# Rows that stay on chip in round three, scatters dealt out by ticks, and one transpose moved ahead of the last batch norm

## The chip, the cores and the metric

The kernel runs on one core of one Trainium2 chip. Its time is the device time of one execution in microseconds, here the median of the runs shown. A second kind of number is the time of one execution under the hardware profiler; that execution is the one that the profile shows, instruction by instruction.

## The reference

The input is x of shape (16, 1024, 128) in float32, a symmetric 0/1 adjacency of shape (16, 1024, 1024) with ones on its diagonal, and a node mask that is all ones. Two layers follow one another, both added to x:

```python
h = jnp.maximum(_layernorm(x, axis=-1), 0.0)
x = x + _L0_gnn_ref(h, adj, ...)        # masked attention: relu(softmax(q k^T on the edges) v Wo + bo)
h = jnp.maximum(_layernorm(x, axis=-1), 0.0)
x = x + _L1_gnn_ref(h, adj, nodemask, ...)
...
adj_d = _dilate(adj, mask)               # row by row, drops most edges of a node
h1 = _bn(relu(_sage(x, adj_d, Wr1, Wx1, b1, mf)), g1, be1)
h2 = _bn(relu(_sage(h1, adj_d, Wr2, Wx2, b2, mf)), g2, be2)
h3 = _bn(relu(_sage(h2, adj_d, Wr3, Wx3, b3, mf)), g3, be3)
return concatenate([h1, h2, h3]) @ Wl + bl
```

`_sage` takes the mean over the kept neighbours, multiplies by Wr, adds x Wx + b and divides each row by its norm. `_bn` normalises each of the 128 features over all 16 x 1024 rows. So there are three rounds, each needs the statistics of the whole round before it, and the last product needs those of round three.

## The kernel before

The work falls into four stages. A general path behind a flag is never taken with these inputs.

**Attention and dilation** come first and end at about 830 us of the profiled span. Beside the attention of one batch the dilation of the graph is solved. It finds the few nodes of a batch that keep any neighbour (at most 256 of 1024) and gives every node a slot, so that the nodes that keep neighbours come first. The 1024 rows of each batch are written to DRAM in the order of the slots, by eight indirect DMAs of 128 rows, and each row carries its node number along. `enter` (L861) reads that number into the tile `nodes`, with one small GpSimd copy for each batch (L864).

**Rounds one and two** then work on batches in slot order, feature by row (a batch is [128 features, 1024 rows]). Everything of round one is kept on the chip in eight tiles `r1` of two batches each, and that of round two in eight tiles `r2`. One batch is one run of the generator `mix` (L913): it makes the neighbour part for the first 256 rows (L918, L921), two half-batches of x Wx (`wx_half`, L937 and L938), adds the neighbour part (L956, L957), squares and sums (L947, L948), and scales by the norm (L959, L960, L963, L966). `turn` (L971) transposes the result back on TensorE (L976), ScalarE takes the relu (L982), and VectorE takes the statistics (L983). The transposes of one batch are issued during the next batch. `batchnorm` (L988) turns the statistics into scaled weights after each round, and `pieces` makes a row of bias for TensorE.

**Round three** does the same, and three things more, in the order that `in_turn` (L1009) is given by hand: `["mix", "thirds", "mix", "mix", "turn", "mix", "thirds", "turn"]`. After each of these eight items the clock ticks once, and what was put off with `later(n, ...)` is issued n ticks on. `thirds` multiplies the rows of rounds one and two by their thirds of Wl (L1114, L1115, into the PSUM tile `ph`), and VectorE adds x (tile `x2`, loaded by `load_rows` at L1100) and writes the sum into the second half of each row of the tile `y` (`add`, L986). The first half of `y` holds what `mix` gave (L966). `scatter_rows` then sends each group of 128 rows, both halves, 1024 bytes a row, to DRAM at the place of its node: eight indirect DMAs for a batch (`scatter`, L533, tile `y_d`), issued by GpSimd, one for each tick from the second tick after the batch. An `engine_nop` on GpSimd follows each. There are three buffers of `y`, so that batch b can start to fill its own only when the scatters of batch b-3 have been carried out. `load_back` (L1106) brings a batch back in node order into the same memory (`r2`, then `r1`): batch b/2 - 1 at every even b, and the last nine after the round, all on the queue of SyncE.

**The last product** follows the batch norm of round three. For every batch `raised` (L1155, L1160) transposes the first half of its rows and takes the relu, `final` multiplies it by the last third of Wl (L1167), adds the bias (L1168), VectorE adds that to the second half (L986 again), and SyncE stores the batch (L1171). The transposes of a batch are issued beside the product of the batch before it. Those of the first batch are issued after `batchnorm(2)` and `pieces` in program order.

```python
y = own.tile([P, NB, 2 * D], F32, name="y")
parts = {"mix": mix(b, r2[b // 2][:, b % 2, :], wxs, wrs, bias, rbias, y[:, :, :D]),
         "thirds": thirds(b, y)}
...
in_turn(["mix", "thirds", "mix", "mix", "turn", "mix", "thirds", "turn"], parts)
scatter_rows(b, y)
prev = (b, y[:, :, :D], None)
```

Of the kernel before, what the change touches and what calls it, by code (L numbers as in the profile page):

```python
# [15 lines left out]
P = 128  # L16
# [20 lines left out]
LAST = 12  # L37
GROUP = 4
# [473 lines left out]
def fast(ctx: ExitStack, tc: tile.TileContext, a, out, vp):  # L512
# [18 lines left out]
    def scatter(dst, slots, src, group):  # L531

        d = nc.gpsimd.indirect_dma_start(out=dst, out_offset=bass.IndirectOffsetOnAxis(ap=slots, axis=0),  # L533
                                         in_=src, in_offset=None)
        tc.declare_no_dep(d.ins, group=group, reason="the rows go to different places")
        tc.add_to_no_dep_group(group, d.ins)
        nc.gpsimd.engine_nop()
# [97 lines left out]
    with ExitStack() as s1:  # L635
# [225 lines left out]
        def enter(b):  # L861

            xt = XT.pop(b)
            nc.gpsimd.tensor_copy(nodes[:, b, :], xt[:, :, D].bitcast(I32))  # L864
# [48 lines left out]
    def mix(b, hT, wxk, wrk, bias, rbias, ob, on_scalar=False):  # L913
# [26 lines left out]
        def squares(g):  # L940
# [7 lines left out]
            later(2, lambda: nc.vector.tensor_reduce(n[:, 0, 4 * g:4 * g + 4], sq, axis=AX.X, op=OP.add))  # L948
# [31 lines left out]

    def put_off(b, g, pt, d):
        later(1, lambda: nc.scalar.activation(d, pt, AF.Relu))  # L982
        later(2, lambda: nc.vector.bn_stats(stats[:, 2 * b + g, :], d))  # L983

    def add(z, first, more):
        later(1, lambda: nc.vector.tensor_add(z, first, more))  # L986
# [83 lines left out]
    with big:  # L1070
# [20 lines left out]

        with tc.tile_pool(name="w3", bufs=3, reuse_waits="tile") as own:
# [3 lines left out]
            X2, R = {}, {}  # L1096
# [5 lines left out]
            def load_back(b):  # L1102

                R[b] = (r2 if b < B // 2 else r1)[b % (B // 2)].rearrange("p a n -> p (a n)").rearrange(
                    "p (k d) -> p k d", d=2 * D)
                nc.sync.dma_start(R[b], y_d[b].rearrange("(k p) d -> p k d", p=P))  # L1106

            def thirds(b, y):

                for g in range(2):  # L1110
# [5 lines left out]
                    add(y[:, 4 * g:4 * g + 4, D:], X2[b][:, 4 * g:4 * g + 4, :], pz)  # L1116
                    yield

            def scatter_rows(b, y):

                for k in range(NB):
                    later(2 + k, lambda k=k: scatter(y_d[b], nodes[:, b, k:k + 1], y[:, k, :], f"y_{b}"))
# [4 lines left out]
            for b in range(B):  # L1127
                if 0 < b < B - 1:
                    later(2, lambda b=b: load_rows(b + 1))
                if b % 2 == 0 and b:  # L1130
                    later(3, lambda b=b: load_back(b // 2 - 1))
                y = own.tile([P, NB, 2 * D], F32, name="y")
                parts = {"mix": mix(b, r2[b // 2][:, b % 2, :], wxs, wrs, bias, rbias, y[:, :, :D]),
                         "thirds": thirds(b, y)}
                if prev:
                    parts["turn"] = turn(*prev)
                in_turn(["mix", "thirds", "mix", "mix", "turn", "mix", "thirds", "turn"], parts)
                scatter_rows(b, y)
                prev = (b, y[:, :, :D], None)
            clock.flush()  # L1140
            drain(turn(*prev))
            clock.flush()
            for b in range(B // 2 - 1, B):
# [3 lines left out]
        (wl2,), pr = batchnorm(2, [wl[:, 2, :]])  # L1147
        bias, = pieces("pc3", [(zrow, pr[:, 0, :])], few)
        tall = big.enter_context(tc.tile_pool(name="w4", bufs=2, reuse_waits="tile"))

        def raised(b, hT):
            for g in range(2):
                pt = ps.tile([P, 4, P], F32, name="pt")
                for k in range(4):
                    nc.tensor.transpose(pt[:, k, :], R[b][:, 4 * g + k, :D], identf)  # L1155
# [3 lines left out]
        def raise_half(h, pt):  # L1159
            later(1, lambda: nc.scalar.activation(h, pt.rearrange("p a b -> p (a b)"), AF.Relu))  # L1160

        def final(b, h):
            for g in range(2):
# [5 lines left out]
                add(R[b][:, 4 * g:4 * g + 4, D:], R[b][:, 4 * g:4 * g + 4, D:], pz)  # L1169
                yield  # L1170
            later(2, lambda: nc.sync.dma_start(out[b].rearrange("(k p) d -> p k d", p=P), R[b][:, :, D:]))  # L1171

        h = tall.tile([P, N], F32, name="hT")
        drain(raised(0, h))
        clock.flush()
        for b in range(B):
            parts = {"final": final(b, h)}
            if b + 1 < B:
                h = tall.tile([P, N], F32, name="hT")
                parts["raised"] = raised(b + 1, h)  # L1180
            in_turn(["raised", "final", "raised", "final"], parts)
        clock.flush()
    return dil.flag
# [584 lines left out]
```

## Time and profile before

| what | us |
|---|---|
| median of 3 runs | 1262.63 (1258.08 to 1264.05) |
| the profiled execution, as a run | 1343.16 |
| its span in the profile | 1341.1 |
| attention, dilation and round one end at (first step of the batch norm) | about 940 |
| round two, until its batch norm | about 940 to 1038 |
| round three, from its first product to the batch norm after it | 1047.2 to 1269.9 |
| last product, first to last VectorE addition's end | 1278.6 to 1333.6 |
| end of the span | 1341.1 |

The profiled execution is 80.5 us longer than the median, so that its durations are those of a longer run than the one that is measured.

The page names a group of instructions by line, engine, operation, what it writes and what it reads, then how many there were, their busy time, the mean length of one in nanoseconds, and the idle time of their engine just before them with what ended most of it. "issue" means that nothing that the profile shows was waited for, and "remote" or "another core or an unknown queue" that the semaphore that ended the wait can't be tied to an instruction. TensorE has two rows, PE for products and PEld for the loading of weights. In a view of stretches of time, PEclk is the share of TensorE's full clock that was granted.

### The profile page before, as it was taken

Reading aid. Unit: us, or ns where it says so; the run is one execution under the profiler, and the core shown is the slowest. Engines: PE = TensorE matmul, PEld = TensorE weight load, DVE = VectorE, ACT = ScalarE, POOL = GpSimd, SP = SyncE. Lnnn points to the kernel's source line nnn. Section 1 sums busy time; section 2 is a strip of 40 time slices with the busy share of each in tenths; the row PEclk is TensorE's granted clock in tenths of the full one; section 3 lists DMA queues with packets and bytes.
Section 4 is the critical chain, followed back from the end, with each engine's and each line's share of the span. In section 5 each row is a group of like instructions: output and inputs, shape, how many; then the busy total and the mean of one; then the engine's idle time right before and its main releaser. Section 6 shows DMA issues by size and latency. Waiting matters only on the chain.

```text
span 1341.1 us, 22234 instructions
## 1 busy us (share of the span) xinstructions
PE 1138.2 (85%) x7815; PEld 854.3 (64%) x7815; DVE 882.6 (66%) x2630; ACT 732.2 (55%) x1580; POOL 548.1 (41%) x961
## 2 busy tenths in 40 slices
PE   4899899998899998998997976987798777777597
PEld 2577566666666666765665665765676666666585
DVE  6668567768776777767777785988587433434443
ACT  5578677767667776766776424665355212222232
POOL 0222464454445536426436156961000255555500
PEclk9899999999999998989999997998799788888899
DMA  6534334333334342433343014220000254444594
GB/s 211 151 121 127 110 119 135 127 111 115 122 111 131 123 143 91 130 123 95 115 125 108 21 52 112 82 65 1 0 1 20 80 163 147 150 146 150 173 342 142
DMA packets 117745, 153.92 MB, mean 115 GB/s; under 512 B 9196, under 2 KB 93048, under 8 KB 117624
## 3 DMA queue, kind: packets, MB, share of 16 engines
q1 hardware_dynamic: 105080, 118.65, 29.0%
q0 software_dynamic: 12544, 33.77, 7.4%
q8 instruction: 63, 1.03, 0.3%
q14 instruction: 58, 0.48, 0.1%
HBM read 118.63 MB, written 33.75 MB: 114 GB/s over the span
## 4 chain that ended last, share of the span: by engine, by line
PE 51%; DVE 23%; ACT 7%; issue 6%; POOL 5%; another core or an unknown queue 5%; DMA 3%; SPq 0%; POOLq 0%; DVEq 0%; ACTq 0%
PE ps L691 9%; PE po L707 9%; PE pm L670 6%; PE po L937 5%; DVE e L694 3%; DMA rows<-in_adj_dram,row 3%; PE ph L1167 2%; PE ph L1114 2%; DVE stats L983 2%; PE pt L976 2%; ACT e L693 2%; DVE left L304 2%; PE ph L1115 2%; PE pm L678 2%
## 5 line engine op out<-in xcount | busy, mean ns | idle before, releaser
L707 PEld LDWEIGHTS po<-vw,e 128*128 128x128 f32 x2048 | 276.4, 196 | 67.4 <-issue 67.0
L707 PE MATMUL po<-vw,e 128*128 128x129 f32 x2048 | 310.2, 286 | 0.0
L691 PE MATMUL ps<-qT,kT 128*128 128x512 f32 x512 | 273.4, 617 | 0.8 <-ACT e L693 0.8
L694 DVE TENSOR_TENSOR e<-e,ab 128x512 f32<-128x512 f32 x256 | 177.7, 695 | 125.3 <-ACT e L693 113.6
L533 POOL DMA_INDIRECT y_d<-y,nodes x128 | 123.2, 963 | 236.2 <-DVE y L966 193.3
L693 ACT ACTIVATE e<-ps 128x512 f32<-128x512 f32 x256 | 153.2, 598 | 120.3 <-PE ps L691 92.3
L533 POOL DMA_INDIRECT x_d<-xt,slot x128 | 141.7, 1107 | 38.7 <-issue 35.1
L166 ACT ACTIVATE ab<-st,d_one_k 128x1024 bf16<-128x1024 f32 x128 | 147.0, 1149 | 0.0
L570 POOL TENSOR_SCALAR ln_t<-ln_st 128x8 f32<-128x8 f32 x31 | 8.0, 259 | 289.3 <-DVE ln_st L563 232.0
L176 ACT ACTIVATE junk<-st 128x1024 bf16<-128x1024 f32 x112 | 118.4, 1057 | 0.0
L1114 PE MATMUL ph<-ws,r 128*128 128x128 f32 x256 | 63.5, 336 | 46.7 <-DVE y L986 45.7
L947 ACT ACTIVATE sq<-po 128x512 f32<-128x512 f32 x80 | 47.7, 596 | 88.2 <-PE po L938 67.2
L716 ACT ACTIVATE o<-po,recips 128x128 f32<-128x128 f32 x128 | 46.8, 368 | 73.3 <-DVE recips L714 69.7
L691 PEld LDWEIGHTS ps<-qT,kT 128*128 128x128 f32 x512 | 79.3, 195 | 7.6 <-issue 3.1
L1114 PEld LDWEIGHTS ph<-ws,r 128*128 128x128 f32 x256 | 49.3, 239 | 53.9 <-DVE y L986 48.5
L986 DVE TENSOR_TENSOR y<-x,ph 128x512 f32<-128x512 f32 x32 | 22.0, 688 | 89.4 <-remote 65.9
L937 PE MATMUL po<-ws,r 128*128 128x128 f32 x512 | 79.6, 303 | 0.0
L937 PEld LDWEIGHTS po<-ws,r 128*128 128x128 f32 x512 | 69.8, 211 | 12.7 <-issue 10.9
L582 POOL TENSOR_SCALAR hn<-xt,ln 128x128 f32<-128x128 f32 x120 | 76.4, 648 | 1.6
L948 DVE TENSOR_REDUCE nrm<-sq 128x4 f32<-128x512 f32 x80 | 54.1, 676 | 34.0 <-ACT sq L947 20.3
L191 DVE SCALAR_TENSOR_TENSOR junkv<-pd,ab 128x64 bf16<-128x64 int32 (+7 forms) x128 | 57.8, 452 | 18.2 <-PE pd L185 12.4
L582 POOL TENSOR_SCALAR hn<-xt 128x128 f32<-128x128 f32 x112 | 57.8, 528 | 27.1 <-PE pt L592 26.6
(292 smaller groups left out, 2382.4 us busy)
## 6 DMA issues: line engine op xcount, KB each, us to landing
st<-in_adj_dram SPq DMA_DIRECT2D x128, 512.0 KB
r<-y_d SPq DMA_DIRECT2D x16, 1024.0 KB
xt<-x_d SPq DMA_DIRECT2D x16, 524.0 KB
xt<-in_x_dram SPq DMA_DIRECT2D x16, 512.0 KB
x<-x_d SPq DMA_DIRECT2D x16, 512.0 KB
out_dram<-r SPq DMA_DIRECT2D x16, 512.0 KB
x_d<-xt,slot POOLq DMA_INDIRECT x128
y_d<-y,nodes POOLq DMA_INDIRECT x128
```

The lines of the kernel that those rows point to most:

```text
L166: nc.scalar.activation(ab[:, k, :], st, AF.Exp, bias=self.one_k, scale=ONE_K, accum_out=self.deg[:, b, k:k + 1])
L176: nc.scalar.activation(junk, st, AF.Exp, scale=-ZERO_K, accum_out=zeros)
L191: nc.vector.scalar_tensor_tensor(junk.rearrange("p a b -> p (a b)")[:, :n], pt.rearrange("p a b -> p (a b)").bitcast(I32)[:, :n], 1.0, ab[ ...
L533: d = nc.gpsimd.indirect_dma_start(out=dst, out_offset=bass.IndirectOffsetOnAxis(ap=slots, axis=0), in_=src, in_offset=None)
L582: engine.tensor_scalar(hn[:, k, :], xt[:, k, :D], minus[:, k // 2, k % 2, None], rstd[:, k // 2, k % 2, None], op0=OP.add, op1=OP.mult)
L670: nc.tensor.matmul(pp, w, hT[:, 512 * g:512 * g + 512], start=True, stop=True)
L691: nc.tensor.matmul(p, K[b][:, k * P:(k + 1) * P], Q[b][:, c], start=True, stop=True)
L693: later(1, lambda: nc.scalar.activation(e, p, AF.Exp))
L694: later(2, lambda: nc.vector.tensor_mul(e, e, AB_[b][:, k, c]))
L707: nc.tensor.matmul(po[:, q % 2, :], E[k][:, i * P:(i + 1) * P], V[b][:, k, :], start=(k == 0), stop=(k == NB - 1))
L937: nc.tensor.matmul(po[:, i, :], hT[:, c:c + P], wxk, start=(i == 3), stop=False)
L1114: nc.tensor.matmul(pz[:, i, :], r1[b // 2][:, b % 2, c], wl0, start=True, stop=False)
```

## The change

- Five batches, 2, 5, 8, 11 and 14 (`STAY`), are not scattered in round three. Their relu from `turn` goes into their part of `r2` in slot order, feature by row, and the sum of `thirds` into their part of `r1`. They are neither loaded back nor transposed again. In the last product their result is scattered straight to the output by eight indirect DMAs of 512-byte rows each. For these batches `nodes` holds the node number plus b times 1024, by `tensor_scalar` in place of the copy.
- The other eleven are scattered to `y_d` as before. `load_back` now fetches batch b-3 during batch b, in two DMAs of 512-byte pieces, into that batch's own part of `r2` and of `r1`.
- A scatter is no longer put off by a fixed number of ticks: it is put into a list, and `pace_scatters`, called after each tick, issues the first of the list if it is due and the number of the tick is no multiple of three. Ahead of each such scatter GpSimd copies one column from `last[0]`, a view of what VectorE wrote last in program order, into the tile `mark`. What is left in the list after the last tick is issued without that copy.
- In the last product the order of batches is 2, 0, 1, 5, 3, 4, 8, 6, 7, 11, 9, 10, 14, 12, 13, 15, and the transposes of batch 0, the first that needs any, stand ahead of `batchnorm(2)` in program order.

```diff
--- before.py
+++ after.py
@@ -35,6 +35,7 @@
 TICKS = 6 * NB
 GROUPS = ((0, 4, 5 * TICKS, 8 * TICKS), (4, 8, 9 * TICKS, 13 * TICKS), (8, 12, 13 * TICKS, 16 * TICKS))
 LAST = 12
+STAY = (2, 5, 8, 11, 14)
 GROUP = 4
 AB = 2
 ST = 3
@@ -528,12 +529,17 @@
     ones3 = consts.tile([3, P], BF, name="ones3")
     nc.vector.memset(ones3, 1.0)
 
-    def scatter(dst, slots, src, group):
+    def apart(d, own, *others):
+        for group in others:
+            tc.declare_no_dep(d.ins, group=group, reason="the rows go to different places")
+        tc.add_to_no_dep_group(own, d.ins)
+    def scatter(dst, slots, src, group, *others):
 
         d = nc.gpsimd.indirect_dma_start(out=dst, out_offset=bass.IndirectOffsetOnAxis(ap=slots, axis=0),
                                          in_=src, in_offset=None)
-        tc.declare_no_dep(d.ins, group=group, reason="the rows go to different places")
-        tc.add_to_no_dep_group(group, d.ins)
+        apart(d, group, group, *others)
         nc.gpsimd.engine_nop()
 
     def load_const(name, shape, src):
@@ -861,7 +867,8 @@
         def enter(b):
 
             xt = XT.pop(b)
-            nc.gpsimd.tensor_copy(nodes[:, b, :], xt[:, :, D].bitcast(I32))
+            nc.gpsimd.tensor_scalar(nodes[:, b, :], xt[:, :, D].bitcast(I32), float(b * N if b in STAY else 0), None, op0=OP.add)
             hT = work.tile([P, N], F32, name="hT", bufs=3)
             hn = work.tile([P, NB, D], F32, name="hn")
             halves = lambda c: xt[:, :, c].rearrange("p (a t) -> p a t", t=2)
@@ -945,7 +952,12 @@
                         sq[:, i, :], halves[g][:, i, :], AF.Square, accum_out=n[:, 0, 4 * g + i:4 * g + i + 1]))
                 return
             later(1, lambda: nc.scalar.activation(sq, halves[g], AF.Square))
-            later(2, lambda: nc.vector.tensor_reduce(n[:, 0, 4 * g:4 * g + 4], sq, axis=AX.X, op=OP.add))
+            def reduce():
+                nc.vector.tensor_reduce(n[:, 0, 4 * g:4 * g + 4], sq, axis=AX.X, op=OP.add)
+                last[0] = n[:, 0, 4 * g:4 * g + 1]
+            later(2, reduce)
 
         wx_half(1)
         squares(1)
@@ -978,12 +990,22 @@
             put_off(b, g, flat, flat if dst is None else dst[:, 512 * g:512 * g + 512])
             yield
 
+    last = [stats[:, 0, 0:1]]
     def put_off(b, g, pt, d):
+        def sums():
+            nc.vector.bn_stats(stats[:, 2 * b + g, :], d)
+            last[0] = stats[:, 2 * b + g, 0:1]
         later(1, lambda: nc.scalar.activation(d, pt, AF.Relu))
-        later(2, lambda: nc.vector.bn_stats(stats[:, 2 * b + g, :], d))
+        later(2, sums)
 
     def add(z, first, more):
-        later(1, lambda: nc.vector.tensor_add(z, first, more))
+        def one():
+            nc.vector.tensor_add(z, first, more)
+            last[0] = z[:, 0, 0:1]
+        later(1, one)
 
     def batchnorm(k, weights):
 
@@ -1089,11 +1111,30 @@
             clock.flush()
 
 
+        tall = lambda b: r2[b // 2][:, b % 2, :]
+        blocks = lambda t: t.rearrange("p (k d) -> p k d", d=D)
+        rows_r = lambda b: blocks(r2[b // 2][:, b % 2, :])
+        rows_z = lambda b: blocks(r1[b // 2][:, b % 2, :])
+        mark = few.tile([P, 1], F32, name="mark")
+        waiting, ticks3 = [], 0
+        def pace_scatters():
+            nonlocal ticks3
+            ticks3 += 1
+            if ticks3 % 3 and waiting and waiting[0][0] <= ticks3:
+                nc.gpsimd.tensor_copy(mark, last[0])
+                waiting.pop(0)[1]()
         with tc.tile_pool(name="w3", bufs=3, reuse_waits="tile") as own:
             (wxs, wrs, wl1), pr = batchnorm(1, [wx[2], wr[2], wl[:, 1, :]])
             bias, rbias = pieces("pc2", [(bs[2], pr[:, 0, :]), (None, pr[:, 1, :])], few)
             zrow = add_row(zrow, pr, 2)
-            X2, R = {}, {}
+            X2 = {}
 
             def load_rows(b):
                 X2[b] = own.tile([P, NB, D], F32, name="x2", bufs=2)
@@ -1101,11 +1142,11 @@
 
             def load_back(b):
 
-                R[b] = (r2 if b < B // 2 else r1)[b % (B // 2)].rearrange("p a n -> p (a n)").rearrange(
-                    "p (k d) -> p k d", d=2 * D)
-                nc.sync.dma_start(R[b], y_d[b].rearrange("(k p) d -> p k d", p=P))
-
-            def thirds(b, y):
+                if b not in STAY:
+                    for i, rows in enumerate((rows_r, rows_z)):
+                        nc.sync.dma_start(rows(b), y_d[b].rearrange("(k p) d -> p k d", p=P)[:, :, i * D:i * D + D])
+            def thirds(b, z):
 
                 for g in range(2):
                     pz = ps.tile([P, 4, P], F32, name="ph")
@@ -1113,13 +1154,12 @@
                         c = slice((4 * g + i) * P, (4 * g + i + 1) * P)
                         nc.tensor.matmul(pz[:, i, :], r1[b // 2][:, b % 2, c], wl0, start=True, stop=False)
                         nc.tensor.matmul(pz[:, i, :], r2[b // 2][:, b % 2, c], wl1, start=False, stop=True)
-                    add(y[:, 4 * g:4 * g + 4, D:], X2[b][:, 4 * g:4 * g + 4, :], pz)
+                    add(z[:, 4 * g:4 * g + 4, :], X2[b][:, 4 * g:4 * g + 4, :], pz)
                     yield
 
             def scatter_rows(b, y):
-
                 for k in range(NB):
-                    later(2 + k, lambda k=k: scatter(y_d[b], nodes[:, b, k:k + 1], y[:, k, :], f"y_{b}"))
+                    waiting.append((ticks3 + 2, lambda k=k: scatter(y_d[b], nodes[:, b, k:k + 1], y[:, k, :], f"y_{b}")))
 
             load_rows(0)
             load_rows(1)
@@ -1127,37 +1167,43 @@
             for b in range(B):
                 if 0 < b < B - 1:
                     later(2, lambda b=b: load_rows(b + 1))
-                if b % 2 == 0 and b:
-                    later(3, lambda b=b: load_back(b // 2 - 1))
+                if b >= 3:
+                    later(3, lambda b=b: load_back(b - 3))
                 y = own.tile([P, NB, 2 * D], F32, name="y")
                 parts = {"mix": mix(b, r2[b // 2][:, b % 2, :], wxs, wrs, bias, rbias, y[:, :, :D]),
-                         "thirds": thirds(b, y)}
+                         "thirds": thirds(b, rows_z(b) if b in STAY else y[:, :, D:])}
                 if prev:
                     parts["turn"] = turn(*prev)
-                in_turn(["mix", "thirds", "mix", "mix", "turn", "mix", "thirds", "turn"], parts)
-                scatter_rows(b, y)
-                prev = (b, y[:, :, :D], None)
+                in_turn(["mix", "thirds", "mix", "mix", "turn", "mix", "thirds", "turn"], parts, pace_scatters)
+                if b not in STAY:
+                    scatter_rows(b, y)
+                prev = (b, y[:, :, :D], tall(b) if b in STAY else None)
             clock.flush()
-            drain(turn(*prev))
+            for _ in turn(*prev):
+                clock.tick()
+                pace_scatters()
             clock.flush()
-            for b in range(B // 2 - 1, B):
+            while waiting:
+                waiting.pop(0)[1]()
+            for b in range(B - 3, B):
                 load_back(b)
 
 
-        (wl2,), pr = batchnorm(2, [wl[:, 2, :]])
-        bias, = pieces("pc3", [(zrow, pr[:, 0, :])], few)
-        tall = big.enter_context(tc.tile_pool(name="w4", bufs=2, reuse_waits="tile"))
+        talls = big.enter_context(tc.tile_pool(name="w4", bufs=3, reuse_waits="tile"))
 
         def raised(b, hT):
             for g in range(2):
                 pt = ps.tile([P, 4, P], F32, name="pt")
                 for k in range(4):
-                    nc.tensor.transpose(pt[:, k, :], R[b][:, 4 * g + k, :D], identf)
+                    nc.tensor.transpose(pt[:, k, :], rows_r(b)[:, 4 * g + k, :], identf)
                 raise_half(hT[:, 512 * g:512 * g + 512], pt)
                 yield
 
         def raise_half(h, pt):
             later(1, lambda: nc.scalar.activation(h, pt.rearrange("p a b -> p (a b)"), AF.Relu))
+        def scatter_out(b, k):
+            scatter(out.rearrange("b n d -> (b n) d"), nodes[:, b, k:k + 1], rows_z(b)[:, k, :], "out", "stores")
 
         def final(b, h):
             for g in range(2):
@@ -1166,20 +1212,37 @@
                     c = slice((4 * g + i) * P, (4 * g + i + 1) * P)
                     nc.tensor.matmul(pz[:, i, :], h[:, c], wl2, start=(i == 0), stop=False)
                 nc.tensor.matmul(pz.rearrange("p a b -> p (a b)"), ones3, bias, start=False, stop=True)
-                add(R[b][:, 4 * g:4 * g + 4, D:], R[b][:, 4 * g:4 * g + 4, D:], pz)
+                half = rows_z(b)[:, 4 * g:4 * g + 4, :]
+                add(half, half, pz)
+                if b in STAY:
+                    for k in range(4 * g, 4 * g + 4):
+                        waiting.append((ticks3 + 3, lambda k=k: scatter_out(b, k)))
                 yield
-            later(2, lambda: nc.sync.dma_start(out[b].rearrange("(k p) d -> p k d", p=P), R[b][:, :, D:]))
-
-        h = tall.tile([P, N], F32, name="hT")
-        drain(raised(0, h))
+            if b not in STAY:
+                later(2, lambda: apart(nc.sync.dma_start(out[b].rearrange("(k p) d -> p k d", p=P), rows_z(b)), "stores", "out"))
+        order = [b for i in range(0, B - 1, 3) for b in (i + 2, i, i + 1)] + [B - 1]
+        hs = {b: tall(b) for b in STAY}
+        def raise_next(i):
+            b = next((b for b in order[i:i + 2] if b not in hs), None)
+            if b is None:
+                return iter(())
+            hs[b] = talls.tile([P, N], F32, name="hT")
+            return raised(b, hs[b])
+        drain(raise_next(1))
         clock.flush()
-        for b in range(B):
-            parts = {"final": final(b, h)}
-            if b + 1 < B:
-                h = tall.tile([P, N], F32, name="hT")
-                parts["raised"] = raised(b + 1, h)
-            in_turn(["raised", "final", "raised", "final"], parts)
+        (wl2,), pr = batchnorm(2, [wl[:, 2, :]])
+        bias, = pieces("pc3", [(zrow, pr[:, 0, :])], few)
+        for i, b in enumerate(order):
+            parts = {"final": final(b, hs[b]), "raised": raise_next(i + 1)}
+            in_turn(["raised", "final", "raised", "final"], parts, pace_scatters)
         clock.flush()
+        while waiting:
+            waiting.pop(0)[1]()
     return dil.flag
 
 
```

## The prediction

> **What bounds the kernel now.** I read the page's chain of work first, then the groups of lines, then round three and the last product in order of time.
>
> ```profile
> PE 51%; DVE 23%; ACT 7%; issue 6%; POOL 5%; another core or an unknown queue 5%; DMA 3%; SPq 0%; POOLq 0%; DVEq 0%; ACTq 0%
> L533 POOL DMA_INDIRECT y_d<-y,nodes x128 | 123.2, 963 | 236.2 <-DVE y L966 193.3
> L986 DVE TENSOR_TENSOR y<-x,ph 128x512 f32<-128x512 f32 x32 | 22.0, 688 | 89.4 <-remote 65.9
> ```
>
> TensorE leads, but 5% of the chain hangs on semaphores that no instruction explains, and the third row says where: the addition of `thirds` in round three, 65.9 us over 15 waits. One such wait, in order of time:
>
> ```profile
> 1163.67 0.96 POOL L533 DMA_INDIRECT y_d<-y,nodes  x1 [0.30 <-issue]
> 1164.34 0.28 PE L921 MATMUL ph<-pc,ones 3*128 3x256 bf16 x1
> 1164.94 0.96 POOL L533 DMA_INDIRECT y_d<-y,nodes  x1 [0.30 <-issue]
> 1167.41 0.69 DVE L986 TENSOR_TENSOR y<-x,ph 128x512 f32<-128x512 f32 x1 [3.98 <-remote]
> 1167.47 0.58 ACT L982 ACTIVATE pt<-pt 128x512 f32<-128x512 f32 x1 [3.79 <-remote]
> 1168.16 0.49 PE L1114 MATMUL ph<-ws,r 128*128 128x128 f32 x2 [3.53 <-DVE y L986]
> 1169.82 0.96 POOL L533 DMA_INDIRECT y_d<-y,nodes  x1 [3.91 <-DVE y L966]
> ```
>
> TensorE has nothing left to do at 1164.6. VectorE and ScalarE both wait for its products, which ended by 1164, and both start together at 1167.4, half a microsecond after the last scatter's data. The period is 13.75 us (the additions at 1153.67, 1167.41, 1181.18). TensorE's own share is 8.59: two `thirds` of 1.785 each (1161.47 to 1163.26) and the 5.02 of a batch of round two (962.32 to 967.34). GpSimd's is 8 scatters of 0.96 + 0.30, so 10.1.
>
> The last product is TensorE's, end to end; with transposes a half-batch takes 1.80 us (1328.60 - 1326.80, the row before), without 1.41:
>
> ```profile
> 1328.60 0.97 PEld L1167 LDWEIGHTS ph<-ws,hT 128*128 128x128 f32 x8
> 1330.01 0.97 PEld L1167 LDWEIGHTS ph<-ws,hT 128*128 128x128 f32 x8 [0.23 <-issue]
> 1331.42 0.97 PEld L1167 LDWEIGHTS ph<-ws,hT 128*128 128x128 f32 x8 [0.23 <-issue]
> ```
>
> [...] after each wait PEclk is 0.50 for some 3 us, so that the first `thirds` takes 2.9 us (1154.41 to 1157.30) in place of 1.79, and the half-batch behind it 1.6 in place of 1.1. [...] here data still flows until 1166.9, 1 us after the row's end at 1165.9. [...] the trace shows small GpSimd operations of 0.20 us that at times take 1.10, but all 128 scatters of `y_d` within 0.957 to 1.019. [...]
>
> **Which time the sum is made against.** The profiled execution took 1343.2, 80.5 more than the median. Are the waits in the median too? Suppose not. They take 54.0 us of the chain in round three (23.9% of 226 from 1046 to 1272), and the half-clock after them about 1.65 x 15 = 25. Without them round three would be GpSimd's: the addition of batch 15 waits for `y`, so for the scatters of batch 12, which end at 1059.3 + 13 x 10.16 + 1.5 = 1192.9; then come 5.8 us of VectorE's rows for a batch and 3.6 of transposes, relu and statistics, and the batch norm starts at 1202.3 in place of 1269.9, 67.6 earlier. The other unexplained waits of the chain are 60.3 (4.5% of 1341.1) - 54.0 = 6.3. That gives 1269.3; were even GpSimd no bound, the batch norm would start at 1190.7 (1047.2 + 3.0 of half-clock + 16 x 8.59 - 1.7 that the first and last batch lack + 4.8 of tail) and the total be 1257.7. The median, 1262.6, lies between them, 6.7 below the one and 4.9 above the other. The rest of the kernel has no 80 us to give. So I take the waits for a cost of the profiled execution, and everything below for the median.
>
> **The change, part by part.**
>
> *Five batches not scattered.* 40 of 128 scatters leave round three. GpSimd needs 88 scatters and their copies. The price of a copy between two scatters stands in the dilation's own rows:
>
> ```profile
> 804.81 0.97 POOL L533 DMA_INDIRECT x_d<-xt,slot  x1 [0.30 <-issue]
> 805.81 0.20 POOL L864 COPY nodes<-xt 128x8 int32<-128x8 int32 x1
> 806.18 0.98 POOL L533 DMA_INDIRECT x_d<-xt,slot  x1 [0.17 <-issue]
> ```
>
> Start to start it is 1.37 in place of 1.27, since the copy fills a gap. Three batches now hold 16 scatters: 16 x 1.37 = 21.9, against 25.8 of TensorE. Round three becomes TensorE's. Gain: 1202.3 - 1190.7 = 11.6 at most, nothing if GpSimd was no bound before. The median's place between the two cases puts it at 4.9/11.6 of that, 4.9; scatters of late batches that nobody waited for may add some, so I take 7.
>
> *The pacing.* Two scatters in three ticks, so 2.74 us of GpSimd in 3.22. Each copy waits for VectorE's latest write; behind it on GpSimd only scatters are queued. Who waits for those: the `y` of three batches on, and `load_back`. For batches 1, 4, 7, 10, 13 the last scatter falls on tick 8b + 24 and batch b+3 needs `y` at tick 8b + 26, 2.15 us later. The scatter needs a lag of 1.37 behind its neighbour, 1.37 of its own and 1.5 of landing: VectorE then waits about 2 us. It has 8.59 - 5.8 = 2.8 to spare in a batch, and TensorE wants the PSUM tile `ph` of that addition again only five ticks on, so I cost it at nothing; uncovered it is 5 x 2 = 10 us. The range is 0 (a later `y` can't gain anything) to 10.
>
> *Loads.* 11 batches of two 0.5 MB loads for 16 of 1 MB. SyncE issues 22 x 0.36 for 16 x 0.46, hidden (SyncE is idle between). In a TensorE-bound batch 0.5 MB of `x2`, 0.69 of loads and 0.69 of scatters make 220 GB/s; 1272 to 1296 carried 345 to 380, so this hides. `load_back(1)` may wait a microsecond on SyncE for the scatter just named; the next `load_rows` is seven ticks off.
>
> *Stay batches on other engines.* Relu to SBUF 0.60 for 0.58, statistics from SBUF 0.687 for 0.698: nothing. `nodes` by `tensor_scalar`: 16 x about 0.02 to 0.2, hidden in round one, at most 3 us.
>
> *Last product.* Ten half-batches need no transposes: 10 x (1.80 - 1.41) = 3.9. The transposes ahead of the batch norm free TensorE from 1272.8 to 1275.5, but the bias row is there only at 1275.95 (L624), so its first half-batch ends at about 1276.3 in place of 1277.94: 1.6. Together 5.5, if TensorE stays the bound. Against it GpSimd: batch 15's eight scatters run until 8.7 us after the start of the batch norm, then 40 x 1.37 = 54.8, 1.0 of data and 3.6 that before lay between the last data (1337.5) and the end: 68.1 after that start. Before it was 71.2, TensorE now 65.7. So GpSimd ends last, and the gain is 3.1. Bounds: 5.5 down to -2.5 (each scatter like the mean of `x_d`, 1.107, which is 0.14 x 40 = 5.6 more).
>
> **Sum.** 7 + 3.1 = 10.1; 1262.6 - 10.1 = 1252.5, say 1252 (0.8%). The likeliest case's own range is 1245 to 1259. Half a per cent, 6.3 us, is about what can be told from no change.
>
> **Rivals.**
> *TensorE was the bound already (1258).* GpSimd's 0.30 gap may be the profile's too; round three then gives nothing and the last product 5. For it: 1257.7 above lies as near to the median. Against: the gaps are 0.30 wherever scatters follow each other.
> *The waits are real (about 1190).* Then pacing takes away up to 54 + 25, less if some stay: 1182 to 1230. For it: the chain. Against: the 80.5.
> *GpSimd becomes the bound (1273, slower).* Place: the last product and the pairs of scatters. Price: at c us each the end lies 8.7 + 40c + 4.6 after the batch norm's start, 2 us more for each 0.05. The 7 from round three are gone at c = 1.62, and half a per cent is lost from 1.78 on. At c = 2.0: 93.3 - 71.2 = 22 less at most 11.6, so +10. For it: scatters of `x_d` between VectorE's rows took up to 2.39. Against: those of `y_d` never over 1.02.
>
> **Chances.** Forecast 0.42, TensorE already 0.23, waits real 0.12, GpSimd 0.23. Faster: 0.36 of the first, 0.07 of the second, 0.12 = 0.55. Same: 0.06 + 0.16 + 0.02 = 0.24. Slower: 0.21. The range 1230 to 1275 leaves out most of the third case (0.10) and the far part of the fourth (0.09).
>
> **What would show it.** In the profile after: scatters of round three spaced and 88 in number, a period near 8.6 wherever no unexplained wait stands, no half-clock there; 40 scatters to the output about 1.37 apart, the last a few us after the last addition; the first products of the last stage right behind the batch norm's. It is wrong if GpSimd's rows are longer than 1.1 or if TensorE waits for VectorE's addition behind a wait for `y`.

## The result, and the profile after

| where | before | after | ratio, 95% interval |
|---|---|---|---|
| the timing of the change | 1260.17 us (6 runs) | 1249.33 us (6 runs) | 0.9908 [0.9886, 0.993] |

The change takes 10.8 us off, 0.9%; predicted were 10.1 and 1252. The total is right, but two terms of it are wrong in opposite directions, and the reason given for the level it is measured from is wrong. The experiments below fell on three chips, which are not alike, and no number can be read without that: on chip A the kernel before takes 1258 us, on chips B and C about 1346 (1338.5 to 1353.7 in all executions). B was used before and after A, so that the hour doesn't explain it; whether it is the chip itself, or something else that differs there, can't be told. The timing of the change was made where before takes 1260; the profile of before, 1343, looks like those of chips B and C.

The profiled execution after took 1249.27 us (span 1247.5), as its median. Groups of instructions of the profile after:

```profile
L540 POOL DMA_INDIRECT y_d<-y,nodes x88 | 86.4, 982 | 29.0 <-issue 28.5 <-DVE nrm L957 0.5
L540 POOL DMA_INDIRECT out_dram<-r,nodes x40 | 39.3, 981 | 7.2 <-issue 7.1 <-DVE r L1005 0.2
L1005 DVE TENSOR_TENSOR y<-x,ph 128x512 f32<-128x512 f32 x22 | 15.1, 688 | 9.2 <-PE ph L1156 6.7 <-POOL mark L1130 1.6
L1130 POOL COPY mark<-y 128x1 f32<-128x1 f32 x30 | 5.8, 193 | 145.8 <-DVE y L1005 143.0 <-DVE nrm L975 1.8 <-POOLq L543 0.4
```

The addition of `thirds` (third row) waits 9.2 us in all, and none of it is "remote", where before had 65.9. The scatters no longer wait for a batch's `y`. Of the copies' 145.8 us of waits (fourth row) 143.0 are a single one, until the first addition of round three; inside the round 18 of the other 79 copies show a wait for VectorE, of 0.2 to 0.5 us, 6.2 in all. GpSimd in round three, in order of time:

```profile
1099.47 0.99 POOL L540 DMA_INDIRECT y_d<-y,nodes  x1 [0.16 <-issue]
1100.83 0.18 POOL L1130 COPY mark<-stats 128x1 f32<-128x1 f32 x1 [0.37 <-DVE stats L997]
1101.49 0.98 POOL L540 DMA_INDIRECT y_d<-y,nodes  x1 [0.48 <-issue]
1102.50 0.19 POOL L1130 COPY mark<-r 128x1 f32<-128x1 f32 x1
1102.86 0.98 POOL L540 DMA_INDIRECT y_d<-y,nodes  x1 [0.16 <-issue]
1103.86 0.20 POOL L1130 COPY mark<-nrm 128x1 f32<-128x1 f32 x1
1104.50 0.98 POOL L540 DMA_INDIRECT y_d<-y,nodes  x1 [0.44 <-issue]
```

Half of the scatters follow the one before after 1.37 us (1101.49, 1102.86), nearly all others after 1.6 to 2.1. Counting as one train the scatters less than 1.45 us apart, round three of after has trains of one to five until its last batch, whose remainder, 13 scatters, runs past the batch norm; before had trains of eight, a batch each. The stretches of round three (second to third batch norm) in before and in after, with busy time of PE, PEld, DVE, ACT and POOL, TensorE's clock, DMA share and GB/s:

```profile
1038.80:1269.90 231.10, 168.30 (x1078) 149.02 (x1078) 94.68 (x179) 48.53 (x116) 117.68 (x123) 0.85 0.44 140
```

```profile
1021.00:1171.00 150.00, 141.27 (x1081) 124.78 (x1082) 94.62 (x179) 49.51 (x116) 93.97 (x160) 0.96 0.63 185
```

TensorE is busy 141 of 150 us at 0.96 of its clock: it bounds round three now, as predicted. The first row is from a profile like those of chips B and C, so the difference of 81 us is not the gain of the timing. The end of after:

```profile
1171.02 1.02 DVE L1013 BATCH_NORM_AGGREGATE bn<-stats 128x2 f32<-128x192 f32 x1
...
1180.48 0.96 POOL L540 DMA_INDIRECT y_d<-y,nodes  x1 [0.30 <-issue]
1182.85 0.18 POOL L1130 COPY mark<-r 128x1 f32<-128x1 f32 x1 [1.41 <-DVE r L1005]
1183.55 0.98 POOL L540 DMA_INDIRECT out_dram<-r,nodes  x1 [0.52 <-issue]
...
1232.12 0.69 DVE L1005 TENSOR_TENSOR r<-r,ph 128x512 f32<-128x512 f32 x1 [0.72 <-PE ph L1214]
...
1237.68 0.98 POOL L540 DMA_INDIRECT out_dram<-r,nodes  x1 [0.16 <-issue]
```

VectorE is done at 1232.8, GpSimd's last scatter at 1238.66, and the span ends at 1247.5, 8.8 later. In those 8.8 us the trace has two instructions of GpSimd that the view leaves out, INC_SWDGE_SEM from 1240.22 (1.39 us) and DRAIN from 1241.65 (4.98 us). In both before and after the pair runs behind GpSimd's last DMA, and I read it as the closing of GpSimd's DMA queue. In before (1.39 and 4.98 us as well) it ran from 1281.84 on, beside the last product.

### The profile page after: what moved, and what is told of

The parts are those of the page before. It is cut to its first block, busy times and chain, and to the rows that moved or that the text cites. A ratio compares the mean times of both kernels' runs of the same rounds, so it can differ in the third digit from the quotient of the medians.

```text
span 1247.5 us, 22348 instructions
## 1 busy us (share of the span) xinstructions
PE 1101.4 (88%) x7775; PEld 824.0 (66%) x7775; DVE 881.2 (71%) x2630; ACT 727.6 (58%) x1570; POOL 576.8 (46%) x1082
## 5 line engine op out<-in xcount | busy, mean ns | idle before, releaser
L713 PEld LDWEIGHTS po<-vw,e 128*128 128x128 f32 x2048 | 273.2, 194 | 65.8 <-issue 65.3
L713 PE MATMUL po<-vw,e 128*128 128x129 f32 x2048 | 307.0, 284 | 0.0
L540 POOL DMA_INDIRECT x_d<-xt,slot x128 | 144.2, 1127 | 38.8 <-issue 35.1
L540 POOL DMA_INDIRECT y_d<-y,nodes x88 | 86.4, 982 | 29.0 <-issue 28.5
L1000 ACT ACTIVATE r<-pt 128x512 f32<-128x512 f32 x74 | 44.4, 601 | 58.3 <-PE pt L988 58.3
L944 PE MATMUL po<-ws,r 128*128 128x128 f32 x512 | 75.4, 292 | 0.0
L305 DVE TENSOR_TENSOR_SCAN left<-rows 128x1024 f16<-128x1024 f32 x16 | 38.1, 2384 | 51.4 <-DMA rows<-in_adj_dram,row 51.4
L944 PEld LDWEIGHTS po<-ws,r 128*128 128x128 f32 x512 | 64.8, 198 | 12.8 <-issue 11.2
L1130 POOL COPY mark<-y 128x1 f32<-128x1 f32 x30 | 5.8, 193 | 145.8 <-DVE y L1005 143.0
L997 DVE BATCH_NORM_STATS2 stats<-r 128x6 f32<-128x512 f32 x74 | 50.9, 688 | 29.6 <-ACT r L1000 29.2
```

Source lines behind the costliest of these rows:

```text
L713: nc.tensor.matmul(po[:, q % 2, :], E[k][:, i * P:(i + 1) * P], V[b][:, k, :], start=(k == 0), stop=(k == NB - 1))
L944: nc.tensor.matmul(po[:, i, :], hT[:, c:c + P], wxk, start=(i == 3), stop=False)
```

## The experiments

The first batch norm's start, the time from the second batch norm to the third (round three) and that from the third to the end of the span (tail), in us from the traces ("paced" means that the copy into `mark` stands ahead of a scatter):

| chip | kernel | scatters of `y` in round three | first batch norm | round three | tail |
|---|---|---|---|---|---|
| (timing) | after | 88, paced | 923.6 | 149.8 | 76.5 |
| A | after | 88, paced | 927.0 | 150.0 | 74.1 |
| A | after, trains with gap | 88 | 924.1 | 150.0 | 73.6 |
| A | after without the copy | 88 | 922.1 | 149.9 | 75.1 |
| A | none stays | 128, paced | 919.8 | 173.2 | 89.3 |
| B | before, two profiles | 128 | 953.6, 946.6 | 232.3, 229.4 | 70.6, 70.0 |
| B | before, last store on GpSimd | 128 | 947.1 | 231.7 | 75.2 |
| C | before with gap | 128 | 939.6 | 227.1 | 73.2 |
| B | no pacing in round three | 88 | 942.5 | 209.5 | 84.8 |
| B | four stay, no copy | 96 | 951.3 | 213.3 | 84.7 |
| B | four stay | 96, paced | 945.3 | 153.7 | 95.2 |
| C | four stay | 96, paced | 944.3 | 151.6 | 90.9 |

Up to the first batch norm all of these kernels run nearly the same code, so this stretch compares the chips without the change. In it readers of TensorE's results have remote waits in all nine traces of the slower kind (eight on B and C, and the first profile of before), 2.6 to 16.7 us in each, every one of them beside a train of eight scatters of `x_d` (in before these start at most 1.8 us apart, and the waits end 0.8 to 2.4 us after the start of the eighth); in the five traces of A and of the timing, with the same trains, there is none. The longest group in before, with us in total, times, and the longest:

```profile
ACT kT L671 <- remote: 6.6, 4, 3.7
```

Round two, in which GpSimd scatters nothing, takes the same everywhere: 95.2 to 97.2 us on B and C, 95.2 to 97.6 on A and in the timing.

**Before again (chip B), twice.** No edit.

> The kernel before, unchanged, profiled a second time. Theory (the waits of TensorE in round three belong to the profiled execution): the plain time is again about 1260 us, and the profiled execution is again longer than the plain one, by an amount that need not be 80 us; the waits that the profile calls remote lie in round three again, where scatters follow each other without a gap. Rival (the waits are real): a profiled execution without them would have a plain time well under 1260 us, and one with them would be as long as the plain time. It also tells whether the 18 us by which attention and round one were longer in the first profile of before than in the profile of after come back.

> The kernel before, unchanged, profiled once more, in the hope of a profile in which it takes about 1260. Theory (as the prediction modelled before without the waits): no unexplained waits in round three; GpSimd back to back, a period of about 10.16 us a batch, so that from the second to the third batch norm about 163.5 us pass; the last product takes 71 us. Rival (TensorE was the bound already): a period of 8.6 and about 152 us. Where it takes 1346 again, round three takes about 227 us.

Measured: 1353.69 and 1343.3, beside executions of before at 1345.92 us (22 runs, 1338.54 to 1351.66) and 1347.83 (19 runs). Executions on chips A and B are recorded alike, each with its span and granted clock (in before 0.95 to 0.961 on A, 0.932 to 0.941 on B), so the record alone doesn't make the 80 us; the theory falls. There is no profile of before on chip A.

**After again (chip A).** No edit.

> The kernel after, unchanged, beside before once more. The runs so far put before at 1346 us where the first timing had 1260, with the unexplained waits of TensorE's readers in every execution. Theory A (those waits are real wherever before takes 1346, they come from bursts of scatters back to back, and pacing removes them): where before takes about 1346, after takes 1292 to 1302, ratio 0.96 to 0.968, and its round three, first batch norm to last, takes 248 us as in the first profile of after; where before takes 1260, after takes 1249 again. Rival B (the kernel with five batches in slots differs from the one with four): a ratio of 0.99 in both places.

Measured: 1245.36 against 1257.84, ratio 0.9886 [0.9843, 0.9929]: the change is worth 12.5 us there, about as in the timing (10.8). After itself has not run on chip B or C.

**No pacing in round three (chip B).**

```diff
-                    waiting.append((ticks3 + 2, lambda k=k: scatter(y_d[b], ...)))
+                    later(2 + k, lambda k=k: scatter(y_d[b], ...))
```

> The kernel after, but the scatters of y in round three are queued as before, two to five batches' calls later, without ticks and without the copy ahead of each; batches still stay in slots. Theory (fewer scatters free GpSimd, pacing adds nothing): within 3 us of the kernel after, 1246 to 1252 us. Rival one (the waits are real and the pacing is what removes them): back towards the kernel before, 1257 us or more. Rival two (pacing costs TensorE, as the thirds wait for VectorE): 1243 us or less. The profile should show the remote waits again if they come from scatters without gaps.

Measured: 1337.8 against 1345.92, ratio 0.9953 [0.9931, 0.9974]. The first rival holds on this chip. With forty scatters fewer round three is 20 to 23 us shorter, but the waits stay, 24.7 us of "remote" before the additions to `y` alone, and the tail is 14 longer.

**Four stay (chips B and C).** `STAY = (2, 5, 8, 11)`.

> The kernel after with four batches in slots instead of five: 12 batches scatter y in round three (96 instead of 88), and 32 instead of 40 scatters of output follow the batch norm. Theory (the last product ends with GpSimd's train of 1.366 us a scatter): the train is 8 x 1.366 = 10.9 us shorter, VectorE's last addition then ends last, about 62 us after the batch norm's start, with the closing of GpSimd hidden: 1241 to 1245 us. Rival one (GpSimd becomes the bound of round three with 12 scattering batches): no gain or slower, 1249 to 1256 us. Rival two (TensorE ends the last product anyway): within 2 us of the kernel after.

> The kernel after with four batches in slots, beside before once more. Where before takes about 1260: theory (with 32 scatters of output GpSimd's train ends before VectorE's last addition, and its closing lies beside the last product): the last product takes 68 to 71 us from the batch norm instead of 74 to 76.5, so 1238 to 1243, ratio 0.983 to 0.987; rival one (GpSimd on the path in round three): 1246 or more; rival two (TensorE ends it anyway): 1244 to 1250, as the kernel after. Where before takes about 1346: 1293 to 1297 again.

Measured: 1295.06 on B, ratio 0.961 [0.9584, 0.9637]; 1285.85 on C, ratio 0.955 [0.952, 0.9579]. Round three takes 151.6 to 153.7 us, nearly as on chip A, but the tail 20 to 25 us more than before's on B. Two of VectorE's waits in the second, on C:

```profile
DVE r L1005 <- remote: 14.8, 1, 14.8
DVE y L1005 <- PE ph L1156: 7.5, 10, 4.0
```

Its columns are us in total, times, and the longest. The additions to `y` (round three, trains of one to four) have no remote wait. The one of 14.8 us, to `r`, ends 23.6 us after the last batch norm (1216.55 - 1193.0): beside it 21 scatters that were left over run as one train, from 1186.8 to 1213.6. What was expected of the tail where before takes 1260 wasn't tried.

**Four stay, no copy (chip B).**

```diff
-                nc.gpsimd.tensor_copy(mark, last[0])
```

> The kernel after with four batches in slots and no copy ahead of a scatter, the likely best of these edits. Theory: 32 scatters of output at 1.27 us are over long before the last product, so TensorE and VectorE end it and GpSimd's closing lies hidden beside them; where before takes 1258 to 1260: 1238 to 1242 us, ratio 0.984 to 0.988. Rival (12 scattering batches put GpSimd back on the path in round three): 1246 us or more. Where before takes 1346: about 1290, as the kernel with four batches and the copy.

Measured: 1341.11, ratio 0.9948 [0.9931, 0.9964], where the same kernel with the copy takes 1295 and about 1290 was expected. This miss tells most about the pacing. Without the copy, in order of time:

```profile
1125.17 0.97 POOL L540 DMA_INDIRECT y_d<-y,nodes  x1 [0.30 <-issue]
1126.44 0.97 POOL L540 DMA_INDIRECT y_d<-y,nodes  x1 [0.30 <-issue]
1127.00 0.28 PE L928 MATMUL ph<-pc,ones 3*128 3x256 bf16 x1
1127.72 0.97 POOL L540 DMA_INDIRECT y_d<-y,nodes  x1 [0.31 <-issue]
1130.30 0.69 DVE L1005 TENSOR_TENSOR r<-x,ph 128x512 f32<-128x512 f32 x1 [3.54 <-remote]
1130.36 0.58 ACT L1000 ACTIVATE pt<-pt 128x512 f32<-128x512 f32 x1 [3.35 <-remote]
```

The scatters stand two in three ticks in the program, and run 1.27 us apart all the same, in trains of eight: each of these rows starts 0.30 to 0.31 us after the one before it ended, and its idle time is "issue", so that none is seen to wait for anything at its tick. The tick is a place in the program; what cut the trains up is the copy that waits for VectorE (a copy that waits for nothing, below, leaves long trains). Without it the remote waits are back:

```profile
DVE r L1005 <- remote: 30.7, 6, 9.4
DVE y L1005 <- remote: 29.0, 7, 5.5
```

**After without the copy (chip A).** The same edit with five batches in slots.

> The kernel after without the copy ahead of paced scatters: two scatters in three ticks remain, at 1.27 us start to start; the 40 scatters of output are 4 us shorter. Theory A1 (spacing by ticks is the cure): no unexplained waits in round three, and 2 to 4 us faster than the kernel after. Rival A2 (the copy's gap is the cure): the waits return, slower than after by 10 us or more where before takes 1346.

Measured: 1240.81 against 1257.84, ratio 0.9854 [0.9814, 0.9894], 4.6 less than after there, with intervals that overlap. Trains of sixteen, and no remote wait of any engine on this chip:

```profile
1126.31 0.97 POOL L540 DMA_INDIRECT y_d<-y,nodes  x1 [0.30 <-issue]
1127.59 0.97 POOL L540 DMA_INDIRECT y_d<-y,nodes  x1 [0.30 <-issue]
```

**Trains with a wider gap (after's scatters on chip A, before's on chip C).** In both the scatters have their places of before, with a copy of a constant that waits for nothing. The edit as it is against before; on A it stands in the kernel after, in place of the pacing of round three:

```diff
-  later(2 + k, lambda k=k: scatter(y_d[b], ...))
+  later(2 + k, lambda k=k: (nc.gpsimd.tensor_copy(mark, eps), scatter(y_d[b], ...)))
```

> The kernel without pacing (bursts of eight scatters, five batches in slots), but with one GpSimd copy of a constant ahead of each scatter, so that scatters of a burst start 1.37 us apart instead of 1.27, as paced pairs do. Theory A1 (the length of the burst matters, not the gap in it): within 0.4% of the kernel without pacing, ratio to before 0.992 to 0.999 where before takes 1346. Rival A2 (the 0.1 us wider gap is the cure): as the kernel after.

> The kernel before, with one GpSimd copy of a constant ahead of each of the 128 scatters of y, which waits for nothing: the burst of eight stays, its scatters start 1.37 us apart instead of 1.27. Where before takes about 1260: theory (GpSimd's train of scatters bounds round three of before, 8 x 1.27 a batch): 128 x 0.1 = 10 to 13 us slower, ratio 1.007 to 1.011; rival (TensorE bounds it): the copies fill up to 10.96 us a batch, at most 5 slower. Where before takes about 1346: theory (what cures the waits is that each pair of scatters waits for VectorE, as the kernel without that copy showed): within 1% of before; rival (the 0.1 us wider gap cures them): 1290 or less.

Measured: on A 1244.59, ratio 0.9879 [0.9833, 0.9926], the same as after: pacing neither costs nor brings anything in round three of that chip, and what the change gains there comes without it. On C 1340.65, ratio 0.9969 [0.9958, 0.998]: the gap is no cure. The waits of that kernel are still there:

```profile
ACT sq L947 <- remote: 64.3, 6, 12.3
DVE y L986 <- remote: 19.5, 2, 10.8
ACT pt L982 <- remote: 13.2, 5, 3.3
```

**None stays (chip A): pacing alone.** `STAY = ()`, a scatter in each tick, before's order of the last product. The transposes of batch 0 still stand ahead of the batch norm.

> Pacing alone: the kernel after with no batch in a slot, so all 128 scatters of y as before, one in each tick with its copy; the transposes ahead of the batch norm and the order of the last product fall back to those of before. Theory A1 (long bursts cause the waits): GpSimd is never free, 128 scatters at 1.37 make 175 us, so round three is bound by it at about 11 us a batch and the waits may return, as the train has no pause; in all slower than after by 20 to 70 us. Rival A3 (what cures is that scatters follow ticks, whatever their number): no unexplained waits, round three about 175 to 190 us instead of 226, so 30 us or more faster than before where before takes 1346, and about 15 slower than before where it takes 1260.

Measured: 1281.75, ratio 1.019 [1.0146, 1.0235], 24 us slower than before. 128 scatters at 1.366 us are 175 us, and round three takes 173.2. Seventeen scatters still start after the batch norm, and the last product has to wait for them (TensorE for 14.4 us, behind the second row):

```profile
1211.75 0.96 POOL L540 DMA_INDIRECT y_d<-y,nodes  x1 [0.30 <-issue]
1214.26 1.08 ACT L1203 ACTIVATE hT<-pt 128x512 f32<-128x512 f32 x2 [21.39 <-DMA y_d<-y,nodes]
```

The waiting tile, `hT`, has nothing to do with `y_d`. As the code has it, its pool w4 takes over the memory of w3, from which batch 15 is being scattered. After has the same wait, of 8.9 us, but TensorE has other products to do meanwhile.

**Last store on GpSimd (before, chip B).**

```diff
-            later(2, lambda: nc.sync.dma_start(out[b]...))
+            engine = nc.gpsimd if b == B - 1 else nc.sync
+            later(2, lambda: engine.dma_start(out[b]...))
```

> The kernel before, with one edit: batch 15's final store goes to GpSimd's queue instead of SyncE's. It adds no transfer; it makes GpSimd's last transfer the last of the program, so that what GpSimd runs to close its queue (1.39 and 4.98 us in the trace) can't lie beside the last product any more. Theory: 3 to 6 us slower than the kernel before. Rival (the closing instructions only fill time in which the other engines close as well): within 1 us.

Measured: 1354.04, ratio 1.0054 [1.003, 1.0077], so 8 us slower, 4 to 10 by the interval (3 to 6 expected). In its trace the two closing instructions take 1.42 and 5.06 us from 1341.84 on, after VectorE's last addition at 1337.04; its tail is 75.2 for 70 to 71. What the store itself costs on GpSimd's queue is in these numbers too.

## Why the prediction was right, and where it was wrong

**"I take the waits for a cost of the profiled execution": wrong.** They are there in plain executions too, on some chips: on B and C all 68 of before take 1338.5 to 1353.7 us, and the profiles of before on B, which show the waits, take as long (1343.3, 1353.69). The step that failed is "the rest of the kernel has no 80 us to give": it compared one profile with a median as if both came from one place. The level was right by luck: the change was timed where after's profile, and so most likely before, has no such waits. That the profiler makes the waits was the author's assumption, which no trace had shown. Profiling can't alone be the cause: the four traces of chip A were profiled as well and show no remote wait, where the two later profiles of before on B have 60.3 and 57.6 us of them ahead of the additions to `y` alone. Whether it has a part in them on B and C no run here shows.

**The rival "the waits are real" is right on chips B and C.** It priced them at 54 + 25 = 79 us. Round three of the kernel with four batches in slots takes 153.7 on B against before's 229.4 to 232.3, and 151.6 on C. Its time falls by only 51 (1345.92 - 1295.06) and 60 us, since the same waits come up behind the last batch norm and the tail grows by 20 to 25. That after does the same there is likely, and wasn't measured.

**Round three, "so I take 7": mis-sized.** Where before takes 1260.2, its span is 2.1 less (as in its profile), 1258.1. Less 1021.2 up to the second batch norm in after (nearly the same code) and 71.2 of tail, 165.7 is left for its round three; after takes 149.8, so the gain is 15.9. With chip A's numbers the same subtraction gives 165.7 (1255.8 - 1018.9, the mean of its four traces, - 71.2). This is worked out, not seen in a trace, and the 71.2 is taken over from the profile of before, whose tail has no remote wait; two more on B have 70.0 and 70.6. The second batch norm's start differs by 5 us between chip A's traces (1016.9 to 1022.3), so I trust it to some 3 us. The two models were near: 163.5 for GpSimd's bound (1202.3 - 1038.8) and 151.9 for TensorE's (1190.7 - 1038.8). What failed is the discount from 11.6 to 7, 4.6 of the 8.9 missing, by "the median's place between the two cases" (the other 4.3 are the models' 2.2 and 2.1). That place was computed with the profile's attention and round one, which is 18 us longer in it (941.5 for 923.6): those us, and not a bound by TensorE, made the median look low. That GpSimd did bound round three fits with the run in which none stays, where 128 scatters at 1.366 give 173.2; it isn't shown in a trace of before.

**"The pacing ... I cost it at nothing": right for round three, not for the queue behind it.** With and without it round three takes 149.9 to 150.0 on chip A; the 1.6 us that additions to `y` wait for `mark` are hidden. (Where before takes 1346 the pacing brings far more than nothing: 213.3 without, 153.7 with.) Start to start was 1.37, as predicted. But late scatters pile up: batch 15's end 10.4 us after the batch norm's start in place of 8.7.

**Loads, stay batches, `nodes`: nothing, right.** Round three at 150, of which TensorE is busy for 141, leaves little room for a cost.

**Last product, "the gain is 3.1": wrong in sign.** The tail is 76.5 for the 71.2 of before's profile, a loss of 5.3 (74.1, a loss of 2.9, on chip A). That GpSimd ends last was right, and so was the length, 40 x 1.366 = 54.6 for 54.8. Two terms were small. The first scatter to the output starts 12.5 us after the batch norm, not 8.7: the pile of 10.4, and 1.4 in which the copy waits for an addition. And 8.8 us lie behind the last scatter, not 4.6: the closing of GpSimd's queue, which in before hid beside the last product; the run with the last store on GpSimd, 4 to 10 us slower, has it uncovered too. Together 3.8 + 4.2 = 8.0 of the 8.4 that the term is off.

TensorE's own 5.5 came out smaller as well, though GpSimd's end hides it: VectorE's last addition ends 61.8 us after the batch norm's start, in before's profile 63.75. The transposes ahead of the batch norm bring little. Their relu also stands ahead of it on ScalarE, so that the batch norm's square root starts 1.9 us after its first step and not 1.06 (1171.02 and 1269.87; the first two rows are after, the third is before):

```profile
1172.44 0.60 ACT L1203 ACTIVATE hT<-pt 128x512 f32<-128x512 f32 x1 [0.26 <-PE pt L1198]
1172.94 0.28 ACT L1014 ACTIVATE bn<-bn,eps 128x1 f32<-128x1 f32 x1
1270.93 0.29 ACT L992 ACTIVATE bn<-bn,eps 128x1 f32<-128x1 f32 x1 [1.82 <-DVE bn L991]
```

The bias row, which the prediction took for what ends last, is ready 7.1 us after the first step in place of 6.1, and the first addition starts after 7.7 in place of 8.7 (7.9 and 8.8 in the other two profiles of before). No run has this part of the change alone.

So 15.9 - 5.3 = 10.6 stands against 7 + 3.1 = 10.1: two errors, of 8.9 and 8.4, that cancel. The sum came out right by luck. As the 15.9 was found by subtraction, both errors rest on the same 71.2: were before's tail 1 us shorter there, each would be 1 us larger.

**What stays open.** Why readers of TensorE's results wait on B and C (up to 14.8 us) and not on A, and whether the results come late or only the word of them, which no trace here tells apart. The runs show the condition, not the cause. Trains of eight in the first stage and in round three, and of 21 after it, have such waits, and so have those of eight and sixteen with 0.1 us more between the scatters; trains of one to four in round three have one of 0.9 us in two traces. It isn't a sharp line: in the tail on B two waits of 1.6 and 1.7 us stand beside short trains that follow closely on one of eight, and in the tail on C trains of seven and eight have none. Attention and round one take some 20 us more there (939.6 to 953.6 for 919.8 to 927.0). The waits beside `x_d` are a part of it, but 16.7 us is the most that they sum to, and 2.6 the least. No one version is shown to be best on both: five batches without the copy, at 1240.81, is the lowest on A, and four with it, at 1285.85 and 1295.06, the lowest on C and B; neither ran on the other kind of chip.

## What to carry to other kernels

A profile that is 6% longer than the median (1343.2 for 1262.6 here) may come from another chip; profile the same kernel on several before a wait in it is called an artefact or a cost. A place in the program didn't pace GpSimd here (without the copy its scatters ran 1.27 us apart in trains of eight): only a wait did, and it also pushed what was left over to the end (a train of 13 scatters in after, of 21 with four batches in slots on C). What issues the last transfer of a program can also decide whose closing is seen: before with its last store on GpSimd took 4 to 10 us more. And work moved ahead of a batch norm can delay the batch norm on the engine that both use, here its square root from 1.06 to 1.9 us after its first step.

## What was not expected of the hardware

- The kernel before takes 1258 us on one chip and 1346 on two others (7%), each steady within about 1%; round two, without scatters, takes the same on all.
- On the two, readers of TensorE's results wait up to 14.8 us at a time beside long trains of scatters, and cutting the trains up takes the waits of round three away but for one of 0.9 us (151.6 to 153.7 us for 229.4 to 232.3 in before); on the first, trains of 16, 40 and 74 scatters go without such waits.
- After its last transfer GpSimd spends 1.39 + 4.98 us on two instructions in before and after (1.42 + 5.06 with the last store on GpSimd), read here as the closing of its queue.
